# Few-row products of an RWKV-6 block issued as pairs in two halves of the matmul array

## The chip, the cores and the metric

The kernel runs on one core of a Trainium2 chip. A core has engines that run side by side, each with its own stream of instructions: TensorE (PE in the profile; PEld is its weight load, which overlaps the matmuls), VectorE (DVE), ScalarE (ACT), GpSimd (POOL) and SyncE (SP), which issues most of the transfers between memory and the on-chip buffers. Matmul results go to banks of a small memory, PSUM, from which DVE or ACT must take them out before a bank can be used again. The metric is the time on the device in microseconds (us); lower is better.

## The reference

The input x has 32 sequences of 128 steps and 512 channels. The reference is one RWKV-6 block, all in float32. A time mixing: layer norm, a shift by one step, five mixed inputs, projections, a recurrence over the steps in 32 heads of 16 channels, a group norm, a gate and an output projection. Then a channel mixing of the same flavour, with two more mixed inputs and three projections. What the change touches is the start of the time mixing:

```python
xn = _ln(x, ln1_w, ln1_b)
sx = _token_shift(xn, state[:, i1])
xxx = jnp.tanh((xn + sx * maa_x) @ maa_w1).reshape(b, l, 5, 1, EXTRA_MAA)   # EXTRA_MAA = 32
xxx = jnp.matmul(xxx, maa_w2).reshape(b, l, 5, E)                            # E = 512
x5 = xn[:, :, None] + sx[:, :, None] * (maa_stack + xxx)
w = jnp.exp(-jnp.exp(time_decay + jnp.tanh(x5[:, :, 1] @ decay_w1) @ decay_w2))
r = (x5[:, :, 3] @ Wr.T)      # and k from x5[0], v from x5[2], the gate from x5[4]
```

So each of the five mixed inputs is made by a product that sums over only 32 rows (`maa_w2`), and the decay by one that sums over 64 (`decay_w2`).

## The kernel before, in words

**Tiling.** Four sequences make a group of 512 columns (4 x 128 steps); eight groups run one behind the other, overlapped. The 512 channels lie in four tiles of 128 partitions. A product of one 128-channel tile with 512 columns in float32 shows in the profile as two matmul records (two passes), each with its own weight load. "ps" is a pool of four PSUM banks of 512 columns which nearly all products and some scratch values share; "sc" and "acc" hold the recurrence.

**Streams.** Each part of the work is a Python generator that yields operations: `front_mix` (line 394: layer norm, shift, the two products of the low rows, the five mixed inputs), `front_proj` (447: decay, k, r, v), `front_gate` (507), `prep` (528), the recurrence's six streams (631 to 737: POOL makes k v products at lines 665 and 669, DVE scans at 687 and multiplies at 689, PE sums at 722 by transposing matmuls, ACT copies), and `back` (745: group norm, output projection at line 810, second layer norm, channel mixing at 382, 884 and 900). Line 382 is the helper `matmuls` for all 128-channel projections of 512 columns.

**Order.** A planner (class `Plan`, lines 72 to 176) runs all streams against a model of the engines while the program is built, and emits the instructions of each engine in the order that comes out. Each operation names an engine, a duration, what it reads and writes, and the buffers it takes. Among the operations that could start within `EPSILON` of the earliest, `pick` (174) takes the one whose due time is smallest; the due times of each kind of stream are in `DUE` (47), in groups. On the chip every engine then works through its list in that order and waits at semaphores where its data is not there.

**The mixing.** Line 414 multiplies the shifted input by `maa_w1`'s first 128 columns (four inputs of 32 rows each); ACT takes tanh of it into "tha" (420). Line 417 does the last 32 columns, with tanh into 32 rows of the standing tile "thb" (423). For each of the five inputs m and each channel tile e, line 435 multiplies "tha" (or "thb") by a 128-row weight in which all rows but the 32 of input m are zero: 20 products a group. DVE takes each result out by two instructions (440: add `maa_stack` and multiply by sx; 442: add xn, into the tile "mx"). These lie in the same stream, one product behind the matmul.

**The decay.** Line 461 multiplies x5[1] by `decay_w1` (64 output columns), 463 takes tanh into 64 rows, and 469 multiplies these 64 rows by `decay_w2`, four products a group, with two exponentials on ACT (474, 476) behind each. `to_lanes` (384) then moves the result by DMA.

**Small weights.** `constants` (244) loads the small weights by SP's queue: `w1_sb` (251), four slices of `w2p` (253), the last slice of `maa_w2` (254) and `decay_w2` (256) into one tile `dw2m`, and `dw1_sb` (255).

Of the kernel before, what the change touches and what calls it, by code (L numbers as in the profile page):

```python
# [14 lines left out]
P = 128  # L15
# [22 lines left out]
GAP = 0.034  # L38
PE_GAP = 0.04

WINDOW, KEEP, WAKE = 3.41, 0.4, 0.7
LANDING = 2.0
HOP = (0.2, 0.05, 0.05, 0.04, 0.08)
EPSILON = 0.02


DUE = {"rec": (0.073, 0.928), "mix": (-1.183, -0.487), "proj": (-1.108, 0.725), "gate": (-0.487, 0.788), "prep": (11.173, 11.194), "back": (1.114, 2.212), "last1": (-8.358, -8.236), "last2": (1.752, 11.136)}

# [22 lines left out]
class Plan:  # L71
# [64 lines left out]
    def run(self):  # L136
        while self.streams:
# [32 lines left out]
            for b in op.end:  # L170
                (b if isinstance(b, Buf) else new[b]).open = False
            self.advance(st, new)

# [6 lines left out]
def rwkv6_block(ctx: ExitStack, tc: tile.TileContext, x, prev, s0, vecs, u, maa_w1, maa_w2,  # L180
# [19 lines left out]
    def tag(pool, shape, name, bufs):  # L200
# [12 lines left out]
        (big, [P, DH, L], "am", 1), (big, [P, DH, T2], "a", 2), (big, [P, DH, L], "rm", 2),  # L213
        (big, [P, N], "tha", 1), (big, [P, N], "th", 2),
        (big, [P, GB, 6], "stats", 2), (big, [P, GB, 2], "mv", 2), (big, [P, GB], "rstd", 2), (big, [P, GB], "nb", 2),
# [9 lines left out]
    u_sb = const.tile([P, S], F32, name="u_sb")  # L225
    w1_sb = const.tile([P, NE, 5 * XM], F32, name="w1_sb")
    w2p = const.tile([P, 4, E], F32, name="w2p")
    dw1_sb = const.tile([P, NE, XD], F32, name="dw1_sb")

    dw2m = const.tile([P, E], F32, name="dw2m")  # L230
    thb = Buf(const.tile([P, N], F32, name="thb"))
# [6 lines left out]
    nc.gpsimd.memset(mhalf, -0.5)  # L238

    nc.gpsimd.memset(thb.t, 0.0)  # L240
    nc.gpsimd.memset(dw2m, 0.0)
    nc.vector.memset(w2p, 0.0)

    def constants():
        nc.sync.dma_start(out=vec, in_=vecs)
        nc.gpsimd.tensor_scalar(ffn[:, 0, :], vec[:, V_FK, :], -1.0, 1.0, ALU.mult, ALU.add)
        nc.gpsimd.tensor_scalar(ffn[:, 2, :], vec[:, V_FR, :], -1.0, 1.0, ALU.mult, ALU.add)
        nc.gpsimd.tensor_tensor(ffn[:, 1, :], ffn[:, 0, :], vec[:, V_LN2B, :], ALU.mult)
        nc.gpsimd.tensor_tensor(ffn[:, 0, :], ffn[:, 0, :], vec[:, V_LN2W, :], ALU.mult)
        nc.sync.dma_start(out=pv, in_=prev)  # L250
        nc.sync.dma_start(out=w1_sb, in_=maa_w1.rearrange("(c p) o -> p c o", p=P))
        for m in range(4):
            nc.sync.dma_start(out=w2p[m * XM : (m + 1) * XM, m, :], in_=maa_w2[m * XM : (m + 1) * XM, :])
        nc.sync.dma_start(out=dw2m[XD : XD + XM, :], in_=maa_w2[4 * XM : 5 * XM, :])
        nc.sync.dma_start(out=dw1_sb, in_=decay_w1.rearrange("(c p) o -> p c o", p=P))
        nc.sync.dma_start(out=dw2m[0:XD, :], in_=decay_w2)
        for e in range(NE):
            nc.sync.dma_start(out=lanes(u_sb, e), in_=u[e * HE : (e + 1) * HE, :].unsqueeze(0).to_broadcast([GB, HE, S]))
# [6 lines left out]
    def col(v, e):  # L265
        return vec[:, v, e : e + 1]
# [113 lines left out]
    def matmuls(p, w, xin, e, cols=slice(0, N)):  # L380
        for c in range(NE):
            nc.tensor.matmul(p, lhsT=w[:, c, e * P : (e + 1) * P], rhs=xin[:, c, cols], start=(c == 0), stop=(c == NE - 1))  # L382

    def to_lanes(d, name, src, e):

# [8 lines left out]
    def front_mix(g, d):  # L394
# [15 lines left out]
        xnT, sx, xin = yield from layernorm_T(g, xt, None, V_LN1W, V_LN1B, 0, use, ("sx", "mx"), need)  # L410
        d["xin"] = True
        (pm,) = yield Op(PE, 8 * PASS, r=[(xin, None)], w=[(0, None)], alloc=["ps"])
        for c in range(NE):
            nc.tensor.matmul(pm.t, lhsT=w1_sb[:, c, 0 : 4 * XM], rhs=xin[:, c, :], start=(c == 0), stop=(c == NE - 1))
        (pm2,) = yield Op(PE, 8 * PASS, r=[(xin, None)], w=[(0, None)], alloc=["ps"], end=[xin])
        for c in range(NE):
            nc.tensor.matmul(pm2[XD : XD + XM, :], lhsT=w1_sb[:, c, 4 * XM : 5 * XM], rhs=xin[:, c, :],  # L417
                             start=(c == 0), stop=(c == NE - 1))
        (tha,) = yield Op(ACT, 0.6, r=[(pm, None)], w=[(0, None)], alloc=["tha"], end=[pm])
        nc.scalar.activation(tha.t, pm.t, AF.Tanh)  # L420
        yield Op(ACT, 0.6, r=[(pm2, None)], w=[(thb, None)], end=[pm2],
                 need=(lambda: "mixed" in data[g - 1]) if g else None)
        nc.scalar.activation(thb[XD : XD + XM, :], pm2[XD : XD + XM, :], AF.Tanh)

        for m in (1, 0, 3, 2, 4) if g else (1, 0, 2, 3, 4):

            lo, w2 = (tha.t, w2p[:, m, :]) if m < 4 else (thb.t, dw2m)
            x5, late = None, []
            for e in range(NE + 1):
                if e < NE:  # L430
                    if x5 is None:
                        pp, x5 = yield Op(PE, 2 * PASS, r=[(thb, None)], w=[(0, None)], alloc=["ps", "mx"])
                    else:
                        (pp,) = yield Op(PE, 2 * PASS, r=[(thb, None)], w=[(0, None)], alloc=["ps"])
                    nc.tensor.matmul(pp.t, lhsT=w2[:, e * P : (e + 1) * P], rhs=lo, start=True, stop=True)  # L435
                    late.append(pp)
                if e > 0:
                    pp, f = late.pop(0), e - 1
                    yield Op(DVE, 0.75, r=[(sx, None)], w=[(pp, None)])
                    nc.vector.scalar_tensor_tensor(pp.t, pp.t, col(V_MAA + m, f), sx[:, f, :], ALU.add, ALU.mult)  # L440
                    yield Op(DVE, 0.69, r=[(pp, None), (xnT, None)], w=[(x5, f)], end=[pp])
                    nc.vector.tensor_tensor(bt(x5[:, f, :]), bt(pp.t), xnT[:, f * GB : (f + 1) * GB, 1 : L + 1], ALU.add)  # L442
            d["x5", m] = x5
        xnT.open = sx.open = tha.open = False
        d["mixed"] = True

    def front_proj(g, d):
# [12 lines left out]
        for c in range(NE):  # L460
            nc.tensor.matmul(pd[0:XD, :], lhsT=dw1_sb[:, c, :], rhs=x5[:, c, :], start=(c == 0), stop=(c == NE - 1))  # L461
        (dlo,) = yield Op(ACT, 0.6, r=[(pd, None)], w=[(0, None)], alloc=["blk"], end=[pd])
        nc.scalar.activation(dlo[0:XD, :], pd[0:XD, :], AF.Tanh)
        late = []
        for e in range(NE + 1):
            if e < NE:
                (p,) = yield Op(PE, 2 * PASS, r=[(dlo, None)], w=[(0, None)], alloc=["ps"],
                                end=[dlo] if e == NE - 1 else [])
                nc.tensor.matmul(p.t, lhsT=dw2m[0:XD, e * P : (e + 1) * P], rhs=dlo[0:XD, :], start=True, stop=True)  # L469
                late.append(p)  # L470
            if e > 0:
                p, f = late.pop(0), e - 1
                (ev,) = yield Op(ACT, 0.69, r=[(p, None)], w=[(0, None)], alloc=["blk"], end=[p])
# [437 lines left out]
    for g in range(NG):  # L911
        for gen, name, n in ((front_mix, "mix", 75), (front_proj, "proj", 72), (front_gate, "gate", 17),
                             (prep, "prep", 40), (back, "back", 140)):
# [47 lines left out]
```

## Time and profile before

| | us |
|---|---|
| median of 3 runs | 1584.29 (1583.74 to 1585.33) |
| the profiled execution | 1586.62 |
| its span, first to last instruction | 1584.8 |
| PE busy | 1470.4 |
| DVE busy | 1321.9 |
| POOL busy | 919.0 |
| ACT busy | 632.7 |

The mean granted TensorE clock was 0.974. Busy time of PE is the time in which at least one matmul record was open; because matmuls overlap, the spacing of their starts tells more of what one costs than its duration. An idle engine that is not the bound costs nothing; the chain of work that ended last, followed back from the last instruction, tells which engine's work stood on the path. In the profile's lists a group reads: line, engine, operation, result and operands with sizes, count, then busy time and mean duration in ns, then idle time before its instructions and what ended it.

### The profile page before, as it was taken

The page shows a single profiled execution, that of the slowest core. Times are in us where ns is not written, and L with a number is a line of the kernel's source. Part 1 is how long each engine was busy: PE and PEld are TensorE (multiplying, and loading weights), DVE is VectorE, ACT ScalarE, POOL GpSimd, SP SyncE. Part 2 cuts the span into 40 slices and gives each one's busy share as a digit, 9 for nine tenths or more (in the row PEclk, how much of TensorE's full clock was granted, in tenths as well). Part 3 has the DMA queues.
Part 4 walks back from the last instruction along what each step waited for, and adds up shares of the span by engine and source line. Part 5 has one row for each costly group of instructions (what it writes and reads, how often), then busy time and mean ns, then how long its engine had stood idle before and what let it go on. Part 6 is the DMA issues. An engine that isn't in the chain of part 4 may idle for free.

```text
span 1584.8 us, 16299 instructions
## 1 busy us (share of the span) xinstructions
PE 1470.4 (93%) x5216; PEld 771.2 (49%) x5216; DVE 1321.9 (83%) x1702; ACT 632.7 (40%) x1213; POOL 919.0 (58%) x549
## 2 busy tenths in 40 slices
PE   5898799899989999999999999999999999978778
PEld 2344354355544554455554555544544555455444
DVE  5539899999989999989979999888988999697642
ACT  4233243345334352444444343443534443336242
POOL 3027683678746694468654694466843884687400
PEclk9999899999999999999999999999999999988989
DMA  6120232514142231423324232332413233240130
GB/s 216 54 83 24 92 97 74 169 60 127 47 143 80 67 120 51 139 88 98 101 71 139 77 117 75 123 104 64 122 50 113 92 107 95 72 140 27 39 121 27
DMA packets 126790, 146.86 MB, mean 93 GB/s; under 512 B 8080, under 2 KB 76304, under 8 KB 125680
## 3 DMA queue, kind: packets, MB, share of 16 engines
q1 hardware_dynamic: 91888, 129.03, 25.0%
q10 hardware_dynamic: 34816, 16.79, 3.7%
q8 instruction: 41, 0.67, 0.2%
q14 instruction: 45, 0.37, 0.1%
HBM read 94.41 MB, written 17.83 MB: 71 GB/s over the span
## 4 chain that ended last, share of the span: by engine, by line
PE 68%; DVE 17%; POOL 8%; issue 3%; ACT 1%; DMA 1%; SPq 0%; DVEq 0%; POOLq 0%
PE ps L382 26%; PE acc L722 10%; PE ps L435 7%; PE ps L884 7%; PE ps L900 6%; PE ps L810 6%; POOL am L665 5%; DVE sc L687 3%; POOL a L669 3%; DVE rm L689 2%; DVE ps L440 2%; PE ps L469 2%; PE ps L461 1%; DVE mx L442 1%; PE ps L417 1%
## 5 line engine op out<-in xcount | busy, mean ns | idle before, releaser
L665 POOL TENSOR_TENSOR am<-v,k 128x1024 f32<-128x1024 f32 x256 | 615.5, 2404 | 211.9 <-DVE k L564 111.2
L382 PE MATMUL ps<-mx,wt 128*128 128x512 f32 (+1 forms) x1312 | 576.3, 587 | 13.4 <-DVE mx L845 5.1
L669 POOL TENSOR_TENSOR a<-am 128x504 f32<-128x504 f32 x256 | 274.9, 1074 | 305.7 <-DVE sc L687 279.0
L382 PEld LDWEIGHTS ps<-mx,wt 128*128 128x128 f32 x1312 | 244.3, 191 | 288.5 <-issue 265.7
L689 DVE TENSOR_TENSOR rm<-sc,r 128x1024 f32<-128x1024 f32 x256 | 312.5, 1221 | 43.1 <-PE acc L722 30.0
L687 DVE TENSOR_TENSOR_SCAN sc<-sc,a 128x512 f32<-128x512 f32 x256 | 312.9, 1222 | 15.9 <-POOL a L669 13.1
L722 PEld LDWEIGHTS acc<-by_head,rm 128*128 128x128 f32 x2176 | 251.6, 143 | 130.9 <-issue 75.1
L722 PE MATMUL acc<-by_head,rm 128*128 128x128 f32 x2176 | 281.4, 276 | 19.7 <-DVE rm L689 12.8
L640 ACT COPY sc<-w 128x512 f32<-128x512 f32 x256 | 151.0, 592 | 233.3 <-DVE rm L689 181.5
L435 PE MATMUL ps<-tha,w2p 128*128 128x512 f32 x256 | 137.2, 634 | 20.7 <-DVE mx L442 5.9
L440 DVE SCALAR_TENSOR_TENSOR ps<-ps,vec,sx 128x512 f32<-128x512 f32 x160 | 119.8, 749 | 39.3 <-PE ps L435 38.9
L651 ACT COPY a<-st 128x8 f32<-128x8 f32 x256 | 50.9, 203 | 189.4 <-DVE sc L687 173.7
L884 PE MATMUL ps<-wt,mx 128*128 128x512 f32 x256 | 115.4, 593 | 4.2 <-DVE mx L408 2.7
L810 PE MATMUL ps<-wt,mx 128*128 128x512 f32 x256 | 116.6, 604 | 1.4 <-DVE x L819 1.4
L442 DVE TENSOR_TENSOR mx<-ps,xnT 128x512 f32<-128x512 f32 x160 | 110.5, 690 | 5.1
L900 PE MATMUL ps<-wt,ev 128*128 128x512 f32 x224 | 100.8, 592 | 0.0
L501 ACT COPY blk<-ps 128x512 f32<-128x512 f32 x96 | 55.9, 583 | 63.1 <-PE ps L382 62.9
L810 PEld LDWEIGHTS ps<-wt,mx 128*128 128x128 f32 x256 | 47.8, 193 | 59.9 <-issue 53.0
L884 PEld LDWEIGHTS ps<-wt,mx 128*128 128x128 f32 x256 | 47.4, 190 | 60.4 <-issue 59.1
L435 PEld LDWEIGHTS ps<-tha,w2p 128*128 128x128 f32 x256 | 43.1, 198 | 61.4 <-issue 21.3
L343 POOL TENSOR_TENSOR rstd<-rstd,mhalf 128x4 f32<-128x4 f32 (+1 forms) x17 | 16.7, 981 | 93.0 <-DVE rstd L341 92.6
L889 DVE SCALAR_TENSOR_TENSOR ps<-th,ps 128x512 f32<-128x512 f32 x32 | 22.1, 689 | 50.6 <-PE ps L900 47.2
(105 smaller groups left out, 1318.0 us busy)
## 6 DMA issues: line engine op xcount, KB each, us to landing
x<-in_x SPq DMA_DIRECT2D x15, 1024.0 KB
wt<-in_wk SPq DMA_DIRECT2D x8, 1024.0 KB
wt<-in_wr SPq DMA_DIRECT2D x8, 1024.0 KB
wt<-in_wg SPq DMA_DIRECT2D x8, 1024.0 KB
dgate<-blk SPq DMA_DIRECT2D x32, 256.0 KB
wt<-in_wo SPq DMA_DIRECT2D x8, 1024.0 KB
wt<-in_fk SPq DMA_DIRECT2D x8, 1024.0 KB
wt<-in_fr SPq DMA_DIRECT2D x8, 1024.0 KB
```

What stands on the lines that cost most here:

```text
L382: nc.tensor.matmul(p, lhsT=w[:, c, e * P : (e + 1) * P], rhs=xin[:, c, cols], start=(c == 0), stop=(c == NE - 1))
L435: nc.tensor.matmul(pp.t, lhsT=w2[:, e * P : (e + 1) * P], rhs=lo, start=True, stop=True)
L440: nc.vector.scalar_tensor_tensor(pp.t, pp.t, col(V_MAA + m, f), sx[:, f, :], ALU.add, ALU.mult)
L640: nc.scalar.copy(sc.t, d["w01"][:, q : q + 1, :].to_broadcast([P, DH, T2]))
L665: nc.gpsimd.tensor_tensor(am.t, v[:, ds, :], k[:, q : q + 1, :].to_broadcast([P, DH, L]), ALU.mult)
L669: nc.gpsimd.tensor_tensor(a[:, :, 1:T2], am2[:, :, 0 : T2 - 1, 0], am2[:, :, 0 : T2 - 1, 1], ALU.add)
L687: nc.vector.tensor_tensor_scan(scf, scf, a.t.rearrange("p d n -> p (d n)"), 0.0, ALU.mult, ALU.add)
L689: nc.vector.tensor_tensor(pair(rm.t), sc.t.unsqueeze(3).to_broadcast([P, DH, T2, 2]), r2[:, q : q + 1, :, :].to_broadcast([P, DH, T2, 2]), ...
L722: nc.tensor.matmul(acc[:, i, :], lhsT=rm[:, i, :], rhs=by_head, is_transpose=True, start=(q == 0 and i % 4 == 0), stop=(q == S), skip_grou ...
L810: nc.tensor.matmul(p.t, lhsT=att[:, c, b * L : (b + 1) * L], rhs=wot[:, c, :], start=(c == 0), stop=(c == NE - 1))
L884: nc.tensor.matmul(p.t, lhsT=xr[:, c, b * L : (b + 1) * L], rhs=frt[:, c, :], start=(c == 0), stop=(c == NE - 1))
L900: nc.tensor.matmul(p2.t, lhsT=kv[:, c, b * L : (b + 1) * L], rhs=fvt[:, c, :], start=(c == 0), stop=(c == NE - 1))
```

## The change

The few-row products are issued two at a time. A new helper puts two channel tiles of the same input beside each other: one product uses rows 0 to 63 of the array (upper half) and writes one PSUM bank, the other uses rows 64 to 127 (lower half) and writes another bank.

```diff
+    def side_by_side(pp, w, up, low):
+
+        for p, h, t in zip(pp, (slice(0, XD), slice(XD, P)), (up, low)):
+            nc.tensor.matmul(p.t, lhsT=w[h, :], rhs=t[h, :], start=True, stop=True)
```

For this the tanh values must lie in both halves. "tha" becomes two tiles wide; two more tanh instructions on ACT write the same values with the halves exchanged. For the fifth input the weights `w1_sb` hold its 32 columns twice with 32 zero columns between (a POOL copy in group 0), so line 417's product, now of 96 columns, delivers both copies. `dw1_sb` holds `decay_w1` twice, so the product of line 461 has 128 columns. The weights `w2p` and the new `dw2p` hold two channel tiles in their upper and two in their lower rows.

```diff
+        if g == 0:
+            yield Op(POOL, 0.9)
+            nc.gpsimd.tensor_copy(w1_sb[:, :, 6 * XM : 7 * XM], w1_sb[:, :, 4 * XM : 5 * XM])
+            nc.gpsimd.tensor_copy(dw1_sb[:, :, 1, :], dw1_sb[:, :, 0, :])
...
-            nc.tensor.matmul(pm2[XD : XD + XM, :], lhsT=w1_sb[:, c, 4 * XM : 5 * XM], rhs=xin[:, c, :],
+            nc.tensor.matmul(pm2[0 : 3 * XM, :], lhsT=w1_sb[:, c, 4 * XM : 7 * XM], rhs=xin[:, c, :],
...
+        nc.scalar.activation(tha[:, 0, :], pm.t, AF.Tanh)
+        nc.scalar.activation(tha[0:XD, 1, :], pm[XD:P, :], AF.Tanh)
+        nc.scalar.activation(tha[XD:P, 1, :], pm[0:XD, :], AF.Tanh)
```

The loop over the five inputs issues two pairs each. A pair takes both of its banks at once; its two evictions by DVE become a stream of their own, added to the planner at the due time of the pair, and the next pair is held back by the planner until at most one earlier tile is still to be evicted. The decay's four products become two pairs in the same way.

```diff
+        done = [0, 0]
+        def mixed(m, i, pp, x5):
+            for f, p in zip((2 * i, 2 * i + 1), pp):
+                yield Op(DVE, 0.75, r=[(p, None), (sx, None)], w=[(p, None)])
+                nc.vector.scalar_tensor_tensor(p.t, p.t, col(V_MAA + m, f), sx[:, f, :], ALU.add, ALU.mult)
+                yield Op(DVE, 0.69, r=[(p, None), (xnT, None)], w=[(x5, f)], end=[p])
+                nc.vector.tensor_tensor(bt(x5[:, f, :]), bt(p.t), xnT[:, f * GB : (f + 1) * GB, 1 : L + 1], ALU.add)
+                done[1] += 1
...
+            for i in range(2):
+                pp = yield Op(PE, PAIR, r=[(thb, None), (tha, None)], w=[(0, None), (1, None)],
+                              alloc=["ps", "ps"] + ([] if i else ["mx"]), need=lambda: done[1] >= done[0] - 1)
+                side_by_side(pp, w2p[:, m, i * P : (i + 1) * P], up, low)
+                done[0] += 2
+                plan.add(mixed(m, i, pp, x5), plan.due, plan.due + 0.02, 4)
...
+        for i in range(2):
+            pp = yield Op(PE, PAIR, r=[(dlo, None)], w=[(0, None), (1, None)], alloc=["ps", "ps"], end=[dlo] if i else [])
+            side_by_side(pp, dw2p[:, i * P : (i + 1) * P], dlo.t, dlo.t)
```

`PAIR` is the planner's duration for a pair (2.45 of its passes of 0.43 us). The small weights are loaded in halves, the upper by SP's queue and the lower by ACT's, and in another order; their memsets shrink.

```diff
+        for m in (1, 0, 2, 3, 4):
+            for h, queue in enumerate((nc.sync, nc.scalar)):
+                r = h * XD + (XM if m in (1, 3) else 0)
+                queue.dma_start(out=w2p[r : r + XM, m, :].rearrange("r (f p) -> r f p", p=P),
+                                in_=halves(maa_w2[m * XM : (m + 1) * XM, :], h))
```

The due times and the planner's window are other numbers as well, so the order of all streams is planned anew:

```diff
-EPSILON = 0.02
-DUE = {"rec": (0.073, 0.928), "mix": (-1.183, -0.487), "proj": (-1.108, 0.725), "gate": (-0.487, 0.788), "prep": (11.173, 11.194), "back": (1.114, 2.212), "last1": (-8.358, -8.236), "last2": (1.752, 11.136)}
+EPSILON = 0.0397
+DUE = {"rec": (-0.0, 1.1), "mix": (-1.199, -0.678), "proj": (-1.193, 1.513), "gate": (1.096, 1.348), "prep": (0.06, 0.276), "back": (1.128, 2.553), "last1": (-13.962, -9.529), "last2": (6.538, 25.524)}
```

## The prediction

> **What bounds the kernel now.** I read the page's shares and slices first, then busy time by stretch, then the chain that ended last, then the matmul records in order of time.
>
> ```profile
> PE 1470.4 (93%) x5216; PEld 771.2 (49%) x5216; DVE 1321.9 (83%) x1702; ACT 632.7 (40%) x1213; POOL 919.0 (58%) x549
> ...
> PE   5898799899989999999999999999999999978778
> ...
> DVE  5539899999989999989979999888988999697642
> ...
> PE 68%; DVE 17%; POOL 8%; issue 3%; ACT 1%; DMA 1%; SPq 0%; DVEq 0%; POOLq 0%
> ```
>
> PE is near full in nearly every slice and carries 68% of the chain, DVE 17%. The stretches say how close DVE stands (columns: stretch, its length, busy time of PE, PEld, DVE, ACT, POOL, then clock, DMA share and GB/s):
>
> ```profile
> 450.00:500.00 50.00, 44.25 (x150) 20.82 (x149) 48.21 (x69) 20.67 (x35) 21.89 (x14) 0.97 0.35 116
> 500.00:590.00 90.00, 88.48 (x347) 49.60 (x346) 82.38 (x94) 41.83 (x87) 72.45 (x44) 1.00 0.35 108
> ...
> 1380.00:1440.00 60.00, 40.63 (x174) 27.03 (x173) 50.12 (x62) 24.72 (x51) 47.13 (x28) 0.76 0.35 119
> ```
>
> Over 500 to 1380 the same view adds up to 860 us of PE and 786 us of DVE in 880: PE 98%, DVE 89%. Some stretches inside a mixing (450 to 500) are DVE's instead. From 1380 to about 1497 the last recurrence runs at the pace of POOL and DVE (line 665 leads the chain there), so PE time saved pays only before it.
>
> Now the matmuls that change, as groups (busy time, mean ns of one, idle before):
>
> ```profile
> L435 PE MATMUL ps<-tha,w2p 128*128 128x512 f32 x256 | 137.2, 634 | 20.7 <-DVE mx L442 5.9 <-DVE a L615 5.7 <-ACT thb L423 4.4
> L469 PE MATMUL ps<-blk,dw2m 64*128 64x512 f32 x64 | 35.6, 652 | 5.6 <-DVE mx L442 2.6 <-DVE mx L801 2.2 <-DVE x L819 0.8
> L435 PE MATMUL ps<-thb,dw2m 128*128 128x512 f32 x64 | 32.2, 595 | 1.6 <-DVE mx L442 1.6
> L440 DVE SCALAR_TENSOR_TENSOR ps<-ps,vec,sx 128x512 f32<-128x512 f32 x160 | 119.8, 749 | 39.3 <-PE ps L435 38.9
> L442 DVE TENSOR_TENSOR mx<-ps,xnT 128x512 f32<-128x512 f32 x160 | 110.5, 690 | 5.1
> ```
>
> Each product is two records (256 + 64 records for 160 products of the mixing, 64 for 32 of the decay): two passes. Durations overlap, so I price by spacing of starts, from the records in order of time (start, duration, engine, line):
>
> ```profile
> 674.42 1.02 PE L435 MATMUL ps<-tha,w2p 128*128 128x512 f32 x2
> 675.38 1.12 PE L469 MATMUL ps<-blk,dw2m 64*128 64x512 f32 x2
> 676.43 1.09 PE L722 MATMUL acc<-by_head,rm 128*128 128x128 f32 x8
> 677.36 1.02 PE L435 MATMUL ps<-tha,w2p 128*128 128x512 f32 x2
> 678.32 1.12 PE L469 MATMUL ps<-blk,dw2m 64*128 64x512 f32 x2
> 679.37 3.70 PE L810 MATMUL ps<-wt,mx 128*128 128x512 f32 x8
> ```
>
> In the chain eight such passes take 3.44 us: 0.43 us a pass, 0.86 a product. Between full-array products nothing is added. But L435 to the 64-row L469 takes 0.96 us (675.38 less 674.42), and L469 to the next 1.05: entering half the rows costs 0.10 here, leaving them 0.19. Over the whole trace entering costs 0.10 to 0.19 and leaving 0.19 every time; I take 0.35 for a visit, with the 0.06 that the L722 block behind it sometimes loses.
>
> **The change part by part.** All 192 products become 96 pairs on the same 0.43 us passes. What a pair costs is not in this trace.
>
> 1. Passes. Before: 384 x 0.43 = 165 us. Bounds for a pair: 2 passes if the halves run wholly together, 4 if not at all. I take the middle by order: records start in program order, and the upper product's second pass starts 0.43 us behind its first, since it uses the same rows; the lower product stands behind both, so its first pass can at best start with the upper's second: three passes, and two for each further pair that follows directly. The instruction order of the changed kernel has the pairs in 79 unbroken runs (69 single, 7 of two, 2 of three, 1 of seven), so 192 + 79 = 271 passes, 116.5 us: 48.5 less.
>
> 2. Visits to half the array. Before: 25 runs of L469 at 0.35, 8 blocks of L461 (64 columns: 0.16 in, 0.15 out by the same spacings), 8 of L417 (32 columns: 0.10 and 0.12): 13 us. After: 79 runs at 0.35, 27.6 us; L461 becomes 128 columns and falls away; L417 becomes 96 columns, between 0 and its old 0.22 (I take 0: nearest to the full width, and at most 1.8 us in all). Net 14.6 us more.
>
> Sum on PE: 34 us less with three passes, 68 less with two, 14.6 more with four.
>
> [...] No run here shows two row groups at work together.
>
> 3. What of it is on the path. Where PE is the bound, its saving is time until DVE stops it. DVE's work stays (160 evictions at 0.75 + 0.69 us), and 786 of 880 us leaves 94: packed as tightly as PE is (98%), 880 could shrink to about 805. So 34 us (30 of it before the last recurrence) fits, but mixings already led by DVE give less. I take 0.8 of 34: 27 us; of 68, about 0.75: 50.
>
> 4. The separate eviction streams and pairs of banks. A pair takes two of the four "ps" banks at once, and the second waits 1.44 us longer for DVE. Before, PE waited for DVE's line 442 at L435 for only 5.9 + 1.6 us in all; between a gain of that 7.5 and a loss of twice it, I take 0 and keep +15 for the range. Behind a waiting pair PE holds the projections (L382) and the recurrence's transposes (L722), for which ACT and then DVE (line 689, waiting 30.0 us for L722 now) wait.
>
> 5. Two more tanh a group on ACT: 16 x 0.594 us (L420) = 9.5 us. They stand between PE's L414 and the first pair; cover is the L417 block of 3.44 us, against 3 x 0.59. If that cover is gone, 1.2 us a group, 9.5 us at most. ACT is 40% busy.
>
> 6. Group 0 and the small weights. SP issues seven small DMAs after w_sb as before, at about 0.43 us; ACT gets six, 2.6 us (at its own lane issues, 1.07 each, 6.4) from 3.0 us on, before its table load at 6.38 and first work at 11.16: hidden, and about 1 us late if the queue also stalls as SP's did from 4.74 to 6.39. POOL gets two copies (0.4 us each by its L236) ahead of the centering, which sat idle 4.83 us for its weight: hidden. The rows arrive in 512-byte pieces in place of 2 KB, under 0.5 MB, before the first product at 26.89: 0, at worst 1 to 2 us. DVE starts the first eviction at 34.34 us whatever PE does (it does two groups' statistics first), then is the pace: 16 evictions in a row end near 57. PE's idle pieces there (0.7 to 1.6 us each up to 79.33) go partly; this is inside the 27. A risk is the clock: 0.90 granted in 25 to 60 us, so idler PE could cost about 3.
>
> 7. New due times and EPSILON reorder all streams. In the written order PE's work ahead of each group's recurrence falls from group 1 on by 24 to 45 us (three passes), from the last about 31, which is the saving itself; the last 70 rows are alike. I price it at 0, with 10 either way.
>
> Sum: 1586.6 (the profiled execution, of which 1584.8 is span) less 27 is 1559.6. That execution stands 2.3 above the median of 1584.29, so the median falls to about 1558.
>
> **The rivals.**
> *Two passes.* The halves overlap fully, 50 us less: about 1534. For it: nothing ties the rows together but the order of issue. Against it: that order.
> *No overlap.* The change does not do what it says: passes stay at 165 us and the visits are added, 14.6 us on PE's path: about 1599. This is the case on the other side, and it decides from 3.65 passes a pair (14.6 / (96 x 0.43) = 0.35 short of four). For it: 69 of 79 runs are single pairs, each of which pays a visit.
> *The gain is eaten.* PE saves its 34, but DVE in the mixings and the two-bank allocation take 15 to 30 of it back: 1570 to 1584. For it: 450 to 500, where DVE is busy 48.21 of 50 us. Against it: DVE's 89% in the long run.
>
> **How the numbers follow.** Three passes 0.50 (own range 1546 to 1572), two passes 0.20, no overlap 0.17, eaten 0.13. A measurement of this kernel tells 0.2% (3 us) from no change. Faster: 0.50 + 0.20 + most of the eaten (0.08) = 0.78; same 0.05 from the eaten; slower 0.17. The range reaches from part of the two-pass case (1532) to the near edge of no overlap (1595), leaving out about one in ten below and one above.
>
> **What would show it.** Right: in a lone pair the third record starts with the second (within 0.02 us), the fourth 0.43 later, and the next full product about 1.29 + 0.19 us after the first; PE's work by spacings falls from 1417 us (2,592 passes at 0.429, 64 of half that, 2,560 transposes at 0.1085, from eight in 0.87, and 13 of visits) to about 1383; DVE's share rises to 85%. Wrong: third record 0.43 behind the second (no overlap), or with the first (two passes); PE waiting for line 455 by tens of us, or DVE above 95% between 500 and 1350 (eaten); a first recurrence later than before's 122.75 us (the head).

## The result and the profile after

The changed kernel takes 1597.14 us (median of 5 runs, 1591.57 to 1598.86) beside 1585.23 us of the kernel before on the same chip: a ratio of 1.0068, 95% interval [1.0043, 1.0092]. It is 12 us slower between the medians (11 by the ratio); 1558 was forecast, with a range of 1532 to 1595. The profiled execution took 1598.86 us, of which 1597.1 is span.

From the page of the changed kernel: busy time, slices, and the engines' shares of the chain that ended last:

```profile
PE 1448.0 (91%) x5216; PEld 753.9 (47%) x5216; DVE 1325.2 (83%) x1702; ACT 641.2 (40%) x1229; POOL 913.8 (57%) x551
...
PE   4898797789999999999999999999999999987878
...
DVE  4537999988999799987999799997999999788642
...
PEclk8799799989999999999999999999999999998989
...
PE 58%; DVE 28%; POOL 5%; issue 5%; DMA 3%; ACT 1%; SPq 1%; DVEq 0%; ACTq 0%; POOLq 0%
```

PE's busy time fell by 22 us, yet the span grew by 12. DVE now carries 28% of the chain, against 17%, with unchanged work. The first ten slices of the granted clock are lower (8799799989, before 9999899999); over the run it was 0.955, against 0.974.

The stretches shown of before, again, and the long one (start and end, length, busy time of PE, PEld, DVE, ACT, POOL, clock, DMA share, GB/s):

```profile
450.00:500.00 50.00, 48.63 (x191) 26.40 (x190) 47.80 (x56) 21.59 (x39) 37.06 (x21) 1.00 0.22 79
500.00:590.00 90.00, 85.22 (x307) 41.84 (x306) 77.65 (x103) 36.55 (x73) 49.27 (x30) 0.98 0.33 106
1380.00:1440.00 60.00, 49.94 (x210) 29.73 (x208) 52.58 (x64) 20.35 (x44) 46.74 (x28) 0.94 0.38 128
500.00:1380.00 880.00, 846.61 (x3129) 439.51 (x3128) 791.72 (x999) 375.32 (x720) 544.08 (x319) 0.99 0.31 99
```

From 500 to 590 both engines now idle: PE 85.22 of 90 (88.48 before), DVE 77.65 (82.38). The order is a new one, so the same stretch doesn't hold the same work; but over 500 to 1380 it is alike: PE 846.61 of 880 (860.02 before), DVE 791.72 (786.11). Neither is full, so they wait for each other. The groups of the changed lines say where (busy, mean ns | idle before, by releaser):

```profile
L453 DVE SCALAR_TENSOR_TENSOR ps<-ps,vec,sx 128x512 f32<-128x512 f32 x160 | 120.2, 752 | 74.0 <-PE ps L395 73.0
...
L395 PE MATMUL ps<-tha,w2p 64*128 64x512 f32 x256 | 97.2, 700 | 26.7 <-DVE mx L455 16.4 <-ACT thb L445 8.6 <-ACT blk L498 0.8
```

DVE waits 73.0 us for the products (38.9 before), although their cost on PE fell, and PE waits 16.4 us here for the evictions (5.9 before). PE's records at one place of a steady group show both what the change brings and what goes wrong (start, duration, engine, line, records, idle time before):

```profile
888.09 1.13 PE L395 MATMUL ps<-tha,w2p 64*128 64x512 f32 x4
889.15 3.70 PE L834 MATMUL ps<-wt,mx 128*128 128x512 f32 x8
...
897.47 1.12 PE L395 MATMUL ps<-tha,w2p 64*128 64x512 f32 x2
900.17 1.12 PE L395 MATMUL ps<-tha,w2p 64*128 64x512 f32 x2 [1.58 <-DVE mx L455]
901.23 5.40 PE L834 MATMUL ps<-wt,mx 128*128 128x512 f32 x8
906.46 1.04 PE L746 MATMUL acc<-by_head,rm 128*128 128x128 f32 x8
907.43 1.13 PE L395 MATMUL ps<-tha,w2p 64*128 64x512 f32 x4
910.13 3.70 PE L834 MATMUL ps<-wt,mx 128*128 128x512 f32 x8 [1.57 <-DVE mx L455]
913.67 3.60 PE L390 MATMUL ps<-mx,wt 128*128 128x512 f32 x8
917.19 1.13 PE L395 MATMUL ps<-tha,w2p 64*128 64x512 f32 x4
```

The pair at 888.09 is as it should be: four records, and the next full product starts 1.06 us later, two passes (0.86) and the 0.19 for leaving half the array. The pair at 897.47 is torn in two: its lower product starts 2.70 us behind the upper one, after 1.58 us of waiting for DVE's line 455. DVE's records there:

```profile
898.63 0.76 DVE L453 SCALAR_TENSOR_TENSOR ps<-ps,vec,sx 128x512 f32<-128x512 f32 x1 [0.83 <-PE ps L395]
899.43 0.69 DVE L455 TENSOR_TENSOR mx<-ps,xnT 128x512 f32<-128x512 f32 x1
901.34 0.76 DVE L453 SCALAR_TENSOR_TENSOR ps<-ps,vec,sx 128x512 f32<-128x512 f32 x1 [1.22 <-PE ps L395]
...
908.59 0.76 DVE L453 SCALAR_TENSOR_TENSOR ps<-ps,vec,sx 128x512 f32<-128x512 f32 x1 [4.02 <-PE ps L395]
```

The eviction that ends at 900.12 and lets the lower product go is that of the upper product of the same pair: DVE had waited for it until 898.63. Nothing ties a product to its own partner's eviction but a bank in which both stand, and the built program says so: six of the 96 pairs (in group 0 and in groups 2 to 6) have one bank for both products. The same 1.58 us stand before the lower product in five of the six; in the sixth, in group 2, it is 4.63. After that wait PE needs 5.23 us for the eight passes of L834 (3.63 at 889.15), at a granted clock of 0.67, and the product at 910.13 waits 1.57 us for the eviction of the upper product of the pair just ahead. In all, the two products start together (within 0.1 us) in 79 of the 96 pairs; besides the six, eleven in groups 0 and 1 do not, and what holds each of these back is open.

### The profile page after: what moved, and what is told of

Its sections match the earlier page's. It is cut to its first block, busy times and chain, and to the rows that moved or that the text cites. A ratio compares the mean times of both kernels' runs of the same rounds, so it can differ in the third digit from the quotient of the medians.

```text
span 1597.1 us, 16306 instructions
## 1 busy us (share of the span) xinstructions
PE 1448.0 (91%) x5216; PEld 753.9 (47%) x5216; DVE 1325.2 (83%) x1702; ACT 641.2 (40%) x1229; POOL 913.8 (57%) x551
## 4 chain that ended last, share of the span: by engine, by line
PE 58%; DVE 28%; POOL 5%; issue 5%; DMA 3%; ACT 1%; SPq 1%; DVEq 0%; ACTq 0%; POOLq 0%
PE ps L390 24%; PE acc L746 8%; PE ps L834 7%; PE ps L395 6%; PE ps L908 5%; PE ps L924 5%; DVE sc L711 5%; DVE rm L713 4%; POOL am L689 3%; DVE ps L453 2%; DVE ps L619 2%; DVE mx L455 2%; POOL a L693 2%; PE ps L489 1%; DVE rk L627 1%
## 5 line engine op out<-in xcount | busy, mean ns | idle before, releaser
L390 PE MATMUL ps<-mx,wt 128*128 128x512 f32 (+1 forms) x1312 | 586.5, 595 | 26.0 <-DVE rk L627 10.2
L693 POOL TENSOR_TENSOR a<-am 128x504 f32<-128x504 f32 x256 | 271.5, 1061 | 427.1 <-DVE sc L711 407.2
L834 PE MATMUL ps<-wt,mx 128*128 128x512 f32 x256 | 128.9, 653 | 7.3 <-DVE mx L455 6.8
L395 PE MATMUL ps<-tha,w2p 64*128 64x512 f32 x256 | 97.2, 700 | 26.7 <-DVE mx L455 16.4
L908 PE MATMUL ps<-wt,mx 128*128 128x512 f32 x256 | 115.1, 592 | 0.0
L834 PEld LDWEIGHTS ps<-wt,mx 128*128 128x128 f32 x256 | 51.2, 210 | 79.4 <-issue 63.5
L924 PEld LDWEIGHTS ps<-wt,ev 128*128 128x128 f32 x224 | 40.5, 190 | 44.3 <-issue 40.9
L395 PEld LDWEIGHTS ps<-tha,w2p 64*128 64x128 f32 x256 | 25.9, 198 | 73.4 <-DVE mx L455 35.3
```

What stands on the lines that cost most here:

```text
L395: nc.tensor.matmul(p.t, lhsT=w[h, :], rhs=t[h, :], start=True, stop=True)
L693: nc.gpsimd.tensor_tensor(a[:, :, 1:T2], am2[:, :, 0 : T2 - 1, 0], am2[:, :, 0 : T2 - 1, 1], ALU.add)
L834: nc.tensor.matmul(p.t, lhsT=att[:, c, b * L : (b + 1) * L], rhs=wot[:, c, :], start=(c == 0), stop=(c == NE - 1))
L908: nc.tensor.matmul(p.t, lhsT=xr[:, c, b * L : (b + 1) * L], rhs=frt[:, c, :], start=(c == 0), stop=(c == NE - 1))
L924: nc.tensor.matmul(p2.t, lhsT=kv[:, c, b * L : (b + 1) * L], rhs=fvt[:, c, :], start=(c == 0), stop=(c == NE - 1))
```

## The experiments

### First suspects: the loads and DVE's pace

**Seven loads.** The small weights on SP's queue alone, in seven transfers as before; a pair's column tiles become 0 and 2, or 1 and 3, so that a half is one block of columns.

```diff
-        for m in (1, 0, 2, 3, 4):
-            for h, queue in enumerate((nc.sync, nc.scalar)):
...
+        w2h = maa_w2.rearrange("(m q) (h c) -> h q m c", q=XM, h=2)
+        for m0 in (1, 0):
+            for h in range(2):
+                r = h * XD + m0 * XM
+                nc.sync.dma_start(out=w2p[r : r + XM, m0::2, :], in_=w2h[h][:, m0::2, :])
...
```

> The changed kernel with one part changed: its twelve small weight loads on two queues become seven on SP's queue alone, as many as before (the four low inputs two or three at a time, halves as 1 KB pieces; a pair now takes channel tiles 0 and 2, or 1 and 3). In the changed kernel SP waited 5.2 us for a load of ACT's queue before it issued w_sb, at 7.39 us where it was 2.24, and DVE's first eviction came at 38.91 where it was 34.34. Theory H (the head: the late loads cost what the change should have won): first eviction near 34.4 again, TensorE's granted clock in 25 to 100 us back from about 0.75 to over 0.85, time down by 10 us or more, to 1587 or less. Theory D (pairs make PE idle and slow while DVE's evictions set the pace, in every group): first eviction near 34.4, but the time falls by those 4.6 us only, at most 7: 1590 to 1593. If loads are hidden anyway: under 2 us.

Measured: 1588.78 us, ratio 1.0021 [1.0009, 1.0033], between the ranges of the two theories. Some 8 of the 12 us go with the loads by the medians; but the runs of either kernel spread over 7 to 8 us, and their fastest ones differ by 5 (1591.57 and 1586.39). The queues of SP and ACT in the changed kernel show why:

```profile
1.75 0.43 SPq L252 DMA_DIRECT2D pv<-in_prev  x1
7.39 0.38 SPq L254 DMA_DIRECT2D w_sb<-in_maa_w  x1
...
2.21 0.73 ACTq L258 DMA_DIRECT2D w2p<-in_maa_w  x1
```

SP's table of waits in the first 20 us has what it waited for (us in total, times, longest):

```profile
SPq L254 <- DMA w2p<-in_maa_w: 5.2, 1, 5.2
```

That is a `w2p` transfer, and only ACT's queue had issued any by then. The built program gives the transfers of both queues eight semaphores, the signals by which a transfer tells that it has landed; ACT's six take five that are still unused and one of SP's, so SP's fourth transfer needs one that ACT's first still holds. The first eviction starts at 38.91 us instead of 34.34, and at 33.96 with seven loads. The granted clock of the head did not come back, against the first theory (0.75 from 25 to 60 us), and the PE saving was still nowhere to be seen.

**Without overlap.** Both products of a pair in the upper half:

```diff
-        for p, h, t in zip(pp, (slice(0, XD), slice(XD, P)), (up, low)):
+        for p, h, t in zip(pp, (slice(0, XD), slice(0, XD)), (up, up)):
```

> The changed kernel with both products of a pair in the upper half of the rows, so that they cannot overlap; order, banks, evictions and visits stay. It leaves out the lower half's weights and values: two of the four channel tiles of every mixed input and of the decay are computed from the other tile's weights, and the outputs are not the reference's. A pair then takes four passes in place of two, 96 x 0.86 = 82 us of PE work more. If PE is the bound throughout (the prediction's view), 65 us or more longer: over 1655. Theory D: PE has room wherever DVE sets the pace (the head and about half of each group) and the longer pairs keep its clock up, so less than half of it shows, under 40 us: under 1637, with a granted clock above the changed kernel's 0.955. Theory H gives no number here, but is nearer to the first.

Measured: 1635.24 us, ratio 1.0304 [1.0289, 1.0318]: 38 us more, where 82 had been reckoned on PE. PE's busy time rose by 65 (1448.0 to 1513.1); the 17 pairs that didn't start together had no overlap to lose, or less of it. A lone pair now takes 1.91 us to the next product, against 1.06:

```profile
908.84 1.98 PE L395 MATMUL ps<-tha,w2p 64*128 64x512 f32 x4
910.75 3.70 PE L834 MATMUL ps<-wt,mx 128*128 128x512 f32 x8
```

So the overlap is real and worth something, and about half of PE's added time is on the path (38 of 65 to 82). The clock stayed at 0.955, where a rise was expected.

**A shorter eviction**, after and before: the first of the two eviction instructions of the mixing (line 453, or 440) is left out.

> The changed kernel with an eviction of one DVE instruction in place of two: the instruction that adds maa_stack and multiplies by sx (line 453) is left out, so the mixed inputs are wrong and the outputs are not the reference's. 160 x 0.75 = 120 us less on DVE. Theory D: DVE's evictions are what keeps PE from using its shorter pairs, so the time falls by 40 us or more, to 1557 or less, and by at least 20 us more than the same cut gives in the kernel before. Theory H or PE as the bound: at most 20 us, about the same as in the kernel before.

> The kernel before with the same cut: line 440 (add maa_stack, multiply by sx) left out, 120 us less on DVE, outputs not the reference's. PE's work stays 1417 us by spacings and it was 97 to 98% busy from 636 to 995 us, so with PE as the bound the time falls by 5 to 20 us, to 1565 or more. If DVE bounded the kernel before as well, by 40 us or more.

Measured: 1540.43 us (ratio 0.9707 [0.9693, 0.972]), 57 us less than the changed kernel; and 1557.62 us (0.9821 [0.9805, 0.9837]), 28 less than before. 120 us of DVE's work are worth twice as much after the change as before; the second run lies between its two cases. I read this as DVE's pace. That was not the whole of it: a shorter eviction also shortens a wait for a bank. In the trace of the first run the lower product of the torn pair waits 0.78 us, not 1.58, and the eight passes behind it keep 3.54 us.

**A warm head.** In group 0 two products more behind each pair, into the accumulator's bank, which is still unused, on top of seven loads:

```diff
+                if g == 0:
+                    for n in (N, N // 2):
+                        nc.tensor.matmul(fill[:, 0:n], lhsT=ident, rhs=tha[:, 0, 0:n], start=True, stop=True)
```

> The kernel with the loads back on one queue, and in group 0 alone, behind each of the ten pairs of the mixing, two products more (512 and 256 columns, 1.29 us at full clock) into the accumulator's bank, which nothing uses yet; nothing reads them. They add about 13 us of PE work between 32 and 65 us, where PE waits for DVE's evictions of 1.39 us each and its clock was granted at 0.60 (30 to 40), 0.89, 0.62 and 0.70 (60 to 70). Theory C (the clock: a pair is so short that PE idles between two evictions, falls to half speed, and then takes 2.07 us for the next pair and 0.86 us for a pass of the projection behind it): the granted clock of 40 to 70 rises to 0.9 or more, the first copies of y start some 5 to 10 us before 214, the total falls to 1578 to 1585. Theory O (the order: the first group is late because the plan holds prices that the chip does not keep, and the clock only follows the idle time): the first copies of y move by less than 3 us, the total stays within 4 us of 1588.8 or rises by some of the 13 us.

Measured: 1588.2 us, ratio 1.002 [1.0006, 1.0034]. The granted clock rose from 0.75 to 0.85 in 25 to 60 us and from 0.84 to 0.91 in 60 to 100, and DVE's twentieth eviction started at 93.42 us instead of 93.14. So the fillers' own work and what the higher clock gave back cancel at best, and the total stays as theory O has it: the clock of the head is not what ate the gain.

**Cheaper products alone.** The kernel before, with the 160 mixing products on bf16 operands:

```diff
-    w2p = const.tile([P, 4, E], F32, name="w2p")
+    w2p = const.tile([P, 4, E], BF16, name="w2p")
...
-    thb = Buf(const.tile([P, N], F32, name="thb"))
+    thb = Buf(const.tile([P, N], BF16, name="thb"))
```

> The kernel before, with nothing of the change: its order, banks, streams and loads stay, but the 160 products of the mixing (L435) run on bf16 operands (tanh written as bf16, the weights cast once by POOL), so that the rounding of these products is left to bf16. A product becomes one pass, and I expect it at a quarter to a half of 0.86 us: PE's work falls by 69 to 103 us, with DVE's unchanged and no visit to half the array. Theory D (PE and DVE share the bound, since each group's mixing goes at DVE's pace): PE's saving shows to 15 to 40 us, 1545 to 1570, and less per us than the 28 us that 120 us of DVE were worth here. Theory P (PE is the bound, as the prediction had it, with 0.75 of its saving on the path, and only the change's own costs ate the gain): 52 to 77 us less, 1508 to 1533. Theory C adds that PE's granted clock falls from 0.974 to 0.96 or below, and that the saving is under 15 us.

Measured: 1569.52 us, ratio 0.9899 [0.9882, 0.9915]. A product is now one record, and its neighbour starts 0.22 us behind it:

```profile
674.34 0.38 PE L444 MATMUL ps<-tha,w2p 128*128 128x512 bf16 x1
674.56 1.04 PE L731 MATMUL acc<-by_head,rm 128*128 128x128 f32 x8
```

So 160 x 0.64, some 102 us of PE work went by the spacings (74 in busy time), with nothing else of the change, and 16 us came of it. That is 0.16 on the path (0.22 of the busy time), at a granted clock of 0.954 in place of 0.974; how much of the saving the clock took back was not separated. In the old order, with the framework's banks, such a saving of PE buys little.

### The bank

The places where the two kernels part were still open. The plan that the kernel writes keeps four slots for the ps banks and chooses one for each product, but the slot's number goes no further: the tile is asked for by tag, and the framework chooses the bank. Naming the banks makes the plan's choice the real one:

```diff
-        def make():
+        def make(i):
             count[0] += 1
+            if name == "ps":
+                return pool.tile(shape, F32, tag=f"ps{i}", bufs=1, name=f"{name}_{count[0]}")
...
-                b = self.slots[tag][i] = Buf(self.tags[tag][0]())
+                b = self.slots[tag][i] = Buf(self.tags[tag][0](i))
```

It was done to the kernel with seven loads, to the kernel before, and to the changed kernel. (The first expectation names groups 0, 1 and four steady ones for the six pairs; by the traces they are in groups 0 and 2 to 6, counting groups from 0.)

> The kernel with the loads back on one queue, and each of the four ps banks under a name of its own, so that a product lands in the bank that the written plan chose for it. In the built program of the changed kernel and of the one with seven loads, six of the 96 pairs (one in each of groups 0, 1 and the four steady ones) have both products in the SAME bank: the lower one waits until DVE has evicted the upper one. Set against the plan, DVE's evictions of the mixing fall behind only there: in a steady group by 6 to 8 us within one stretch of 20 us, and by nothing elsewhere. Order, loads, pairs and streams stay as in the kernel with seven loads; no pair shares a bank then. Theory B (the shared bank is what ate the gain): the four steady places give 6 to 8 us each and the two early ones up to 5 each, so 26 to 42 us less than 1588.8: 1547 to 1563, and PE's wait for L452's evictions falls by half. Theory D (DVE's pace and the idle clock in every group): less than 10 us, 1579 to 1589.

> The kernel before with each of its four ps banks under a name of its own, and nothing else. Its products are evicted one by one, and against its plan it lost only 0.5 us a group. Theory B: within 4 us of 1585 either way, since no two products belong together here. If it falls by 10 us or more, the naming of banks helps any form of this kernel and says nothing of the pairs.

> The changed kernel as it is, with its twelve loads on two queues, and each ps bank under a name of its own. Theory B: 26 to 42 us less than 1597, so 1555 to 1571, and 6 to 10 us above the run with seven loads and named banks, as the loads cost 8 without it. Theory D: less than 10 us less, 1587 to 1597.

Measured: 1547.45 us (0.9756 [0.9739, 0.9773]), 41 less than with seven loads; 1568.86 us (0.9888 [0.9871, 0.9906]), 18 less than before; 1548.99 us (0.9763 [0.9742, 0.9783]), 48 less than the changed kernel. The first is at the fast end of theory B's range, the third 6 us below it. PE's idle time before these products that DVE's second eviction instruction ended, weight loads counted, fell from 59.8 us with seven loads to 17.4. The second expectation missed: naming helps the kernel before as well, so by its own terms these three runs alone say nothing of the pairs. With named banks the change is worth 20 us (1568.86 to 1548.99). The loads, 5 to 8 us with the framework's banks, are worth 1.5 between the medians here (6 to 10 were expected) and 4.5 between the fastest runs (1542.23 and 1546.69), so their price stays unsettled.

The kernel before with named banks, and the changed kernel with named banks, from their pages, and stretches of the latter:

```profile
PE 1467.4 (94%) x5216; PEld 772.7 (49%) x5216; DVE 1323.2 (84%) x1702; ACT 633.1 (40%) x1213; POOL 919.2 (59%) x549
```

```profile
PE 1425.3 (92%) x5216; PEld 749.7 (48%) x5216; DVE 1322.7 (85%) x1702; ACT 642.5 (41%) x1229; POOL 913.5 (59%) x551
...
PEclk9799898899999999999999999999999999988989
```

```profile
500.00:590.00 90.00, 90.00 (x337) 45.86 (x336) 82.57 (x115) 41.65 (x80) 54.75 (x33) 1.00 0.38 118
500.00:1380.00 880.00, 858.81 (x3242) 451.53 (x3241) 819.04 (x1032) 385.55 (x739) 570.62 (x335) 1.00 0.32 103
```

PE is full again from 500 to 590 (90.00, against 85.22), with DVE at 82.57; over 500 to 1380 PE has 858.81 and DVE 819.04, 93%. The two products start together in 87 of the 96 pairs. The place shown above, in its records:

```profile
866.74 1.13 PE L397 MATMUL ps<-tha,w2p 64*128 64x512 f32 x4
867.80 3.70 PE L836 MATMUL ps<-wt,mx 128*128 128x512 f32 x8
871.34 1.04 PE L748 MATMUL acc<-by_head,rm 128*128 128x128 f32 x8
872.30 1.13 PE L397 MATMUL ps<-tha,w2p 64*128 64x512 f32 x4
873.36 3.70 PE L836 MATMUL ps<-wt,mx 128*128 128x512 f32 x8
876.90 3.60 PE L392 MATMUL ps<-mx,wt 128*128 128x512 f32 x8
880.43 1.13 PE L397 MATMUL ps<-tha,w2p 64*128 64x512 f32 x4
```

The same instructions take 13.69 us (866.74 to 880.43) where they took 19.72 (897.47 to 917.19). The 6.03 us are: 2.70 for the pair torn in two (3.76 instead of 1.06), 1.69 for L834 at a lower clock behind it (5.23 instead of 3.54), and 1.64 for the product that waits for the next pair's upper bank (2.70 instead of 1.06).

The starts of the same eviction of the mixing (160, twenty a group) in four traces, in us:

| eviction | before | before, banks named | after | after, banks named | after less named |
|---|---|---|---|---|---|
| 1 | 34.34 | 34.33 | 38.91 | 38.83 | 0.1 |
| 20 | 86.99 | 78.51 | 98.84 | 87.93 | 10.9 |
| 40 | 218.45 | 207.09 | 224.39 | 210.07 | 14.3 |
| 60 | 358.41 | 345.68 | 396.90 | 378.68 | 18.2 |
| 80 | 550.93 | 538.18 | 575.74 | 551.69 | 24.0 |
| 100 | 737.53 | 723.75 | 759.03 | 727.11 | 31.9 |
| 120 | 921.50 | 907.27 | 940.67 | 903.90 | 36.8 |
| 140 | 1107.14 | 1088.10 | 1123.98 | 1079.34 | 44.6 |
| 160 | 1291.99 | 1272.91 | 1298.22 | 1251.05 | 47.2 |

Within a group the last column is a staircase: it rises by 6.0, 7.7, 6.1 and 7.6 us between evictions 69 and 73, 89 and 93, 109 and 113, 129 and 133, the four places with a shared pair, and stays within 2 us over the rest of those groups: 27.4 of its 47.2 us. In the kernel before, naming the banks moves the last eviction by 19.1 us, 11.4 of them by the 28th.

**Is it the shared pairs, or banks at large?** With named banks and seven loads, three kernels put the framework's choice back step by step: first the lower products of the six pairs into their partner's bank, then the four products of the output projection (L834 above, 910.13) into the bank of the upper product ahead, then twelve early products into a bank used one or two products before. The edit of the second:

```diff
+ONE_BANK = (72, 405, 759, 1052, 1345, 1638)
+BEHIND = (771, 1064, 1357, 1650)
...
+                if count[0] in BEHIND:
+                    u = bank[count[0] - 2]
+                    perm[perm.index(u)], perm[i] = perm[i], u
+                i = bank[count[0]] = bank[count[0] - 1] if count[0] in ONE_BANK else perm[i]
```

> The kernel with seven loads and named banks, and back in one bank only the two products of the six pairs that shared one in the changed kernel (pairs 10, 29, 42, 54, 66 and 78 of 96); all other products stay in the banks of the plan. Naming the banks took 41 us off the kernel with seven loads, but moved other products too, and 17 us off the kernel before, which has no pairs to split. Theory B (the six shared pairs are the price): 24 to 40 us of the 41 come back, 1571 to 1588. Rival M (the many other products that wait for a bank in the framework's own choice, as in the kernel before): under 12 us come back, 1547 to 1559. In between, both.

> The kernel with seven loads, named banks and the six pairs in one bank each, and on top, in each of the four steady groups, one product of the output projection (L831 there) put into the bank of the upper product of the pair just ahead of it, as the changed kernel has it: four products of 580, all else unmoved. Its trace shows such a product waiting 1.57 us for DVE's eviction of that upper product. Six pairs gave back 21 of the 41 us that naming the banks took off. Theory B2 (the same fault in a second place): the four places cost 2 to 4 us each, so 8 to 16 us above 1568.6: 1577 to 1585, and the rest up to 1588.8 lies in the first two groups. Rival M (the rest is spread over the many other products whose bank is not the plan's): under 5 us, 1567 to 1573.

> The same with twelve more of the changed kernel's bank choices, all in groups 0 to 2: products that stand in the bank of one of the two ps products just ahead of them (eight of them pairs' products, behind a pair). Four steady places cost 7.7 us, 1.9 each. Theory B2: the rest lies here, 6 to 13 us above 1576.3: 1582 to 1589. Rival M: under 4 us, up to 1580, and the remaining gap to 1588.8 is spread.

Measured: 1568.6 us (0.9875 [0.9852, 0.9898]), 1576.33 us (0.9933 [0.9921, 0.9945]) and 1582.03 us (0.9981 [0.997, 0.9991]). The first lies between its two ranges, 2 us short of theory B's and 10 above rival M's: by its expectation, both count. The second is just short of B2's range and 3 above its rival's, the third at the low end of B2's and 2 above its rival's. Of the 41 us, the six pairs bring back 21, four products 8, twelve early ones 6; where the last 7 lie is not shown. Each of these steps is uncertain by some 2 to 5 us, by the intervals. The torn pair in the trace with six shared pairs only:

```profile
873.86 1.12 PE L400 MATMUL ps<-tha,w2p 64*128 64x512 f32 x2
876.56 1.12 PE L400 MATMUL ps<-tha,w2p 64*128 64x512 f32 x2 [1.58 <-DVE mx L460]
877.61 3.70 PE L839 MATMUL ps<-wt,mx 128*128 128x512 f32 x8
```

It has the same 2.70 us, but L839 behind it keeps its 3.54 us, at a granted clock of 1.00. With the four products added, the clock falls there too (0.56 from 884.91 to 891.10):

```profile
883.20 1.79 PE L401 MATMUL ps<-tha,w2p 64*128 64x512 f32 x2 [1.58 <-DVE mx L461]
884.91 6.38 PE L840 MATMUL ps<-wt,mx 128*128 128x512 f32 x8
...
894.80 3.70 PE L840 MATMUL ps<-wt,mx 128*128 128x512 f32 x8 [1.57 <-DVE mx L461]
```

**Who sets the pace then?** Named banks and seven loads, with the edit of "without overlap":

> Named banks and seven loads, and both products of each pair in the upper half (the lower halves of the weights and of tanh are left out of the computation), so that they cannot overlap: 2 passes more for each of the 96 pairs, 82 us of PE work. With the shared banks the same edit cost 38 of the 82. Theory P (with the banks out of the way PE sets the pace again, as the prediction's shares of 0.75 to 0.8 had it): 60 to 75 us more, 1607 to 1623. Theory D (PE and DVE take turns): 30 to 50 us more, 1577 to 1597.

Measured: 1602.73 us, ratio 1.0096 [1.0075, 1.0117]: 55 us for 82 us of PE work (84 in busy time, 1420.2 to 1503.8), between the two theories. PE is on the path for two thirds of it, against 38 of 65 to 82 with shared banks.

**Every buffer named**, with seven loads (`tag=f"{name}{i}", bufs=1` for all tags):

> The kernel with seven loads, and every buffer of every tag under a name of its own, not the four ps banks alone, so that SBUF tiles, the sc banks and the DRAM buffers too lie where the written plan put them. If the framework's choice of buffer delays those as well, up to 15 us below 1547.5: 1532 to 1545; if the banks were all there was to it, within 4 us of it.

Measured: 1544.05 us (1539.66 to 1544.72), ratio 0.9722 [0.9701, 0.9744], 3.4 us under named ps banks. That fits both cases, and the two intervals overlap, so it doesn't decide between them. It is the lowest median among the kernels that compute the whole block, 2.8% below the kernel before.

## Why the prediction was wrong

The step that failed is the fourth, the pairs of banks: priced at 0, the banks cost the changed kernel some 30 us more than they cost the kernel before (48 against 18, by naming them), and that turned a gain into a loss. With the banks out of the way the change gains 20 us; the sum without that step had 27.

*Step 1, passes:* wrong in the size, on the safe side. I took three passes for a lone pair, an estimate from the order of issue; no run shows a third: at the full clock, a lone pair of the changed kernel that waits for nothing starts 1.06 us ahead of the next product (all 49 of them), where three passes and the leaving would be 1.48. If all pairs did so, PE's work would fall by 82.6 us and not by 48.5 ahead of the visits, by 68 and not 34 with them; 79 of 96 did, and 87 with named banks. The order of issue is kept: the lower product's first pass starts 0.006 to 0.007 us behind the upper's. What failed is my step from it, that the lower product stands behind both passes of the upper one, whose second starts 0.53 us behind its first. Two passes a pair, the first rival's count, is what the trace shows.

*Step 2, visits:* a lone pair takes 0.20 us more than its two passes to the next full product, as 0.19 for leaving had it; nothing spoke against the 0.35.

*Step 3, what is on the path:* 0.75 to 0.8 was too much. With the banks out of the way, 68 us less of PE work by steps 1 and 2 at most (42 in busy time, 1467.4 to 1425.3) gave 20 us, a share of 0.29 to 0.48; the 102 us taken alone from the kernel before gave 0.16. DVE's 89% from 500 to 1380 was read as room of 75 us; with PE's work cut it went to 93% only. That the room is used up in some stretches and unused in others, because in-order engines wait for each other's single products, is my reading; no run separates it.

*Step 4, separate streams and pairs of banks:* this is the step that turned the sign. I priced it at 0 with up to +15, for a second bank that comes free 1.44 us late. The price was 48 us, by naming the banks, of which the kernel before already paid 18. I had the place and the wait right (PE behind line 455, the projections behind it), but took the banks of the plan for the banks of the program. A pair in one bank doesn't come a little late: it is no pair. It took 3.76 us in one bank, 1.58 of them a wait for DVE's eviction of the upper product, and 1.06 in two.

*Step 5, two more tanh:* nothing spoke against it. PE's one long wait for `thb` is in the head, 8.6 us, and 3.6 with seven loads (4.4 before).

*Step 6, the small weights:* wrong. "Hidden" left out that ACT's loads and SP's share what tells of their landing: SP stalled 5.2 us, the first eviction came at 38.91 and not at 34.34 "whatever PE does", and the loads cost 5 to 8 us in the kernel as changed.

*Step 7, due times:* not separated. The new order is part of the 20 us that the change is worth with named banks.

Of the rivals, "the gain is eaten" had the mechanism in part (the allocation of two banks), but not above the time before. "No overlap", the case on the other side, came out at nearly the time measured, 1599, by luck: its cause didn't occur, since the products of 79 of 96 pairs start together.

What remains open: by what rule the framework chose one bank for two products of one pair, where the last 7 us lie, and why the kernel before gains 18 us, most of it early.

## What to carry to other kernels

When a plan written in the kernel decides when a buffer is free, bind the plan's slot to the physical buffer; otherwise a framework may hand out another one, and products priced as parallel can become serial (3.76 us a pair here, in place of 1.06). A profile shows it as a pair of records split in two with a wait (1.58 us here) that ends when the partner's own eviction ends: compare the places where the same instruction drifts apart in two traces, before blaming an engine's share. A second queue for small loads wasn't free here either (5.2 us of waiting on SP): look at what the first queue waits for.

## What the runs showed of the hardware that was not expected

- Two products of two passes each, in the two row halves and in different banks, take the time of one: 1.06 us from the pair's start to the next full product, against 1.05 for a single 64-row product of the kernel before (678.32 to 679.37) and 1.91 with both in the same half.
- Behind a wait of 1.58 us on PE, as much again went in clock: after the torn pair, eight passes took 5.23 us instead of 3.54, at a granted clock of 0.67. It need not be so: behind the same wait in the kernel with six shared pairs they kept 3.54, at 1.00. In the head of the kernel with seven loads the clock is granted at 0.50 from 57 to 64 us, though PE is busy for 4.84 of these 7 us and idles for 1.26 and 1.44 us; the two passes of one product of a pair take 2.07 us there:

```profile
61.23 2.07 PE L392 MATMUL ps<-tha,w2p 64*128 64x512 f32 x2 [1.44 <-DVE mx L452]
```

- A higher granted clock in the head (0.85 instead of 0.75 from 25 to 60 us), bought with filler products, gained nothing measurable (the warm head, 1588.2 against 1588.8).
- A queue's next load can wait for a transfer that another engine's queue issued, 5.2 us here.
